# Row sums by accumulating DMAs in one layer of a four-layer graph network, and fewer transposes

## The chip, the cores and the metric

The kernel runs on one core of a Trainium2 chip. The metric is the device time in microseconds (us) of one execution. The core has five instruction streams that run side by side, each in its own order: TensorE (PE, matrix products; loading a stationary operand is shown as PEld), VectorE (DVE), ScalarE (ACT), GpSimd (POOL) and SyncE (SP, which here only issues DMAs).

## The reference

32 samples, each with 512 nodes of 256 features in float32, pass four layers over one 512 x 512 adjacency matrix. Each layer normalises its input, applies relu, and adds its result to the input:

```
for layer in (mha, gat1_gat2, gat_heads4, gat_heads8_prior):
    h = maximum(layernorm(x), 0)
    x = x + layer(h, adj)
```

Layer 0 is masked multi-head attention with 4 heads. Layer 1 is two single-head graph attentions between small dense layers. Layers 2 and 3 are graph attentions with 4 heads of 64 features and 8 heads of 32; layer 3 adds a prior to the logits and ends in a dense layer. For each head of layers 2 and 3:

```
e   = leaky_relu(e_src[i] + e_dst[j])         # e_src, e_dst: one number per node and head
att = softmax(where(adj[i, j], e, -inf), over j)
out[i] = sum_j att[i, j] * v[j]
```

So each head needs for every node i a sum over 512 neighbours j of the weights (the row sum), beside the weighted sum of v.

## The kernel before, in words

The tensors on chip are 128 partitions wide. A sample is four row blocks of 128 nodes. A "block" is a 128 x 512 float32 tile in SBUF; 60 of them (`BLOCKS`) are shared by all work, and 8 PSUM banks of the same shape ("bank") by all matmul results.

Nothing is emitted directly. The functions `layer0` to `layer3` only record instructions (in `Plan.add`, L103 and on) with the tiles they touch, an assumed cost from `cost` (L297) and a due time. `Plan.order` (L148) then goes through all 32 samples' instructions as a list scheduler: at each step it takes, over all engines, the instruction that by the assumed costs can start first, with earlier due times first among equals, and it emits them in that order. Several samples are in work at once. What steers it are constants at the head of the file: `PERIOD` (the spacing of due times), `STARTS`, `PACE` and `LAYERS` (the earliest time of a sample and of its layers), `URGENT` (a shift of the due time of single kinds of tile in single layers) and `BLOCKS`. On the chip each engine keeps the emitted order and waits by semaphores. All recorded instructions carry the line number L261, the one that issues them; so groups are told apart by tile names.

PE works in three forms: full 128 x 128 products, "columns" (up to four products of 32 output rows each side by side, recorded as one unit) and "rows" (two products of 64 contracted rows side by side). A float32 product is two matmul records in the trace, a transpose is one.

The places that the change touches:

- `first_gat` (layer 1) needs two projections of each node, source and destination. Four column products `f1p<-o1,fr1a` leave partial results in 128 rows (the two wanted rows of each of four groups of 32 are repeated through the group). ACT copies them to `part`. Four small products against a 128 x 2 selector `pick` then add up the right rows and turn them so that nodes lie on partitions; DVE copies the eight columns to `sd`.
- `separable` serves layers 2 (`nh` = 4) and 3 (`nh` = 8). A product gives v and, in `e`, both per-node numbers of each head. The source numbers of each row block are transposed (4 transposes into `pt`), copied by ACT to `rT` (nh x 512), written by SP to DRAM (`rd`) and read back as `R`, each head's row repeated on all 128 partitions. Then, for a group of four heads and for each block j of 128 neighbours, ACT forms `p = exp(R + e_dst)` (bias), and DVE `p = max(p, exp(e_dst / ALPHA)) * mask`. Each `p[s]` goes into the column unit that forms `av`. Row sums come in two ways: in group 0 (`added`) DVE adds the four j blocks of a head into `total[s]` and one column unit `sm<-total,ones` sums over partitions at the end; in group 1, which only layer 3 has (its last four heads), a second column unit `sm<-p,ones` follows each of the four `av` units and adds up in PSUM.
- `normalise` sends the sums through DRAM to DVE's reciprocal and back, repeated on partitions (`rc`).
- `norm_t`, at the head of each layer, takes the variance plus epsilon (`ve`, DVE) to the power -1/2 on POOL (`rs`), then `ms` on DVE, `h` on ACT, transposes of `h` on PE and `hT` on ACT. POOL's only other work in the loop is `x<-x,boa` in layer 0.

Of the kernel before, what the change touches and what calls it, by code (L numbers as in the profile page):

```python
# [11 lines left out]
F32 = mybir.dt.float32  # L12
BF16 = mybir.dt.bfloat16
I32 = mybir.dt.int32
AF = mybir.ActivationFunctionType
ALU = mybir.AluOpType
AX = mybir.AxisListType
PSUM = bass.MemoryType.PSUM

P = 128  # L20
N = 512
NT = N // P
D = 256
KD = D // P
HID = 512
KH = HID // P
ALPHA = 0.2
# [5 lines left out]
H3, F3 = 8, 32  # L33
# [5 lines left out]

PERIOD = 51.0
STARTS, PACE = (0.0, 8.0, 36.0, 32.0), 110.0
LAYERS = (0.0, 51.0, 151.0, 201.0)

URGENT = {
    "stats:0": 76, "h:0": 358, "mm:0": 3, "sc:0": 60, "p0:0": -99, "av:0": 39, "stats:1": -269, "pt:1": 119,
    "nd:1": -201, "total:1": 12, "av:1": -22, "e:1": -39, "o2:1": 73, "s:1": -189, "pt:2": 15, "e4:2": -44,
    "total:2": 10, "stats:3": -38, "mv:3": -56, "mm:3": -12, "p3:3": -178, "total:3": -169, "sm:3": 86,
    "s1:3": -16,  # L50
}
BLOCKS, KEEP = 60, 2
KEEP_BANKS = 0
BANKS = ("mm", "av", "sm", "sc", "pt", "fb", "f1p")

# [241 lines left out]
def cost(engine, op, args, kw, out):  # L297

    src = next((kw[k] for k in ("in_", "in0") if k in kw), args[1] if len(args) > 1 else out)
    if not isinstance(src, bass.AP):  # L300
        src = out
    n = 1
    for _, k in (src if op in ("bn_stats", "reduce_max") else out).ap[1:]:
        n *= k
    if engine == "PE":
        return (0.109 if op == "transpose" else max(0.224 if n < 3 else 0.0, n * 0.001676)), 0.165
    pointers = sum(isinstance(kw.get(k), bass.AP) for k in ("bias", "scale"))
    if op == "mul":
        pointers = 1
    if engine == "ACT":  # L310
        busy = 0.05 + 0.000832 * n + 0.093 * pointers + (0.0 if src.tensor.name.startswith(BANKS) else 0.043)
        return busy + (0.093 if "accum_out" in kw else 0.0), 0.12
    if engine == "DVE":
        if op == "reciprocal":
            return 0.06 + 0.0062 * n, 0.085
        if op == "tensor_scalar" and n == N:
            return 0.456, 0.075
        by_pointer = op == "scalar_tensor_tensor" and isinstance(args[2], bass.AP)
        return 0.066 + 0.00105 * n + (0.06 if by_pointer else 0.0), 0.085
    if engine == "POOL":  # L320
        return (1.0 if n < 16 else 0.683), 0.1
    size = 4
    for _, k in (out.ap if out.tensor.name.startswith(("few", "R", "rc", "x")) else src.ap):
        size *= k
    return 0.4, 1.6 + size / 190e3
# [3 lines left out]
def gnn_stack_kernel(ctx: ExitStack, tc: tile.TileContext, a: dict, out: bass.AP):  # L329
# [12 lines left out]
    nc = tc.nc  # L342
# [3 lines left out]
    const = ctx.enter_context(tc.tile_pool(name="const", bufs=1))  # L346

    def T(ap, rearr, **kw):
        return ap.rearrange(rearr, **kw)
# [27 lines left out]
    ident = const.tile([P, P], F32, name="ident")  # L377
# [4 lines left out]
    ones = const.tile([P, P], F32, name="ones")  # L382
# [7 lines left out]

    fr1a = const.tile([P, KH, 32], F32, name="fr1a")
    f1a, r1a = fr1a[:, :, 0:1], fr1a[:, :, 1:2]
    pick = const.tile([P, 2], F32, name="pick")

    w2 = const.tile([P, KD, D + 4 * H2], F32, name="w2")
    w3 = const.tile([P, KD, D + 4 * H3], F32, name="w3")
# [10 lines left out]
    with prep_stack, tc.manual_schedule():  # L407
# [11 lines left out]
        for name in ("bq", "bk"):  # L419
            t = prep.tile([1, D], F32, name=f"{name}r")  # L420
# [32 lines left out]
        H = H2 + H3  # L453
        tests = prep.tile([P, 2 * H + 5], F32, name="tests")
        nc.vector.memset(tests, 0.0)
        for c in range(2):
            nc.vector.tensor_reduce(pick[:, c : c + 1], ident[:, c:P:32], axis=AX.X, op=ALU.add)


        top = prep.tile([P, NT], F32, name="top")  # L460
# [4 lines left out]
        for j in range(NT):  # L465
            pt = pp.tile([P, N], F32, name="adjT", bufs=NT)
# [49 lines left out]
        for w, row in zip((wq, wk), rows):  # L516
            gp = pp.tile([64, N], F32, name="gp", bufs=2)
            for h in range(4):
                c = slice(h * 64, (h + 1) * 64)
# [7 lines left out]
        for n in range(2):  # L527
            for h in range(4):
                c = slice(h * 64, (h + 1) * 64)
# [47 lines left out]
        for k in range(KH):  # L577
            for c in range(2):
                pr = prep.tile([P, HID], F32, name="prf")
                nc.vector.tensor_tensor_reduce(  # L580
                    out=pr, in0=wfc[:, k, :], in1=afc[:, c * HID : (c + 1) * HID], scale=1.0, scalar=0.0,
                    op0=ALU.mult, op1=ALU.add, accum_out=fr1a[:, k, c : c + 1],
# [4 lines left out]
        for k in range(KD):  # L587
            for c in range(2):
                pr = prep.tile([P, HID], F32, name="prf")
                nc.vector.tensor_tensor_reduce(  # L590
                    out=pr[:, :D], in0=wh[:, k, :D], in1=ahd[:, c * D : (c + 1) * D], scale=1.0, scalar=0.0,
                    op0=ALU.mult, op1=ALU.add, accum_out=wh[:, k, D + c : D + c + 1],
# [9 lines left out]
    def pipelined(stack):  # L602

        big = stack.enter_context(tc.tile_pool(name="big", bufs=1))
        psum = stack.enter_context(tc.tile_pool(name="psum", bufs=8, space=PSUM))
        dram = stack.enter_context(tc.tile_pool(name="dram", bufs=6, space=bass.MemoryType.DRAM))
        q = Plan(nc, PERIOD)
        def block(name):

            return q.tile(big, [P, N], name, BLOCKS, keep=KEEP, tag="block")  # L610

        def blocks(name, n):
            return [block(name) for _ in range(n)]

        def bank(name):
            return q.tile(psum, [P, N], name, 8, keep=KEEP_BANKS, tag="bank")

        def small(name, *free):
            return q.tile(big, [P, *free], name, 4)
# [5 lines left out]
        def col(t):  # L625
            return slice(t * P, (t + 1) * P)
# [134 lines left out]
        def first_gat(o1):  # L761
# [4 lines left out]
            part, sd = block("part"), small("sd", NT, 2)  # L766
            f1p = bank("f1p")
# [1 line left out]
                for k in range(KH):  # L769
                    q.tensor.matmul(f1p[k * 32 : k * 32 + 32, :], fr1a[:, k, :], o1[k], start=True, stop=True)  # L770
            q.scalar.copy(part, f1p)
            f1p = bank("f1p")
            for t in range(NT):
                q.tensor.matmul(f1p[:, 2 * t : 2 * t + 2], part[:, col(t)], pick, start=True, stop=True)
            q.vector.tensor_copy(T(sd, "p t c -> p (t c)"), f1p[:, : 2 * NT])
            mx = small("mx", 2)
            q.vector.reduce_max(mx[:, 0:1], sd[:, :, 1], axis=AX.X)
            pt = bank("pt")
            q.tensor.transpose(pt[:1, :P], mx[:, 0:1], ident)
            q.vector.reduce_max(mx[:1, 1:2], pt[:1, :P], axis=AX.X)  # L780
            pt = bank("pt")
            q.tensor.matmul(pt[:, 0:1], ones[:1, :], mx[:1, 1:2], start=True, stop=True)
            nd = small("nd", 3)
# [3 lines left out]
            ew = small("ew", 3, NT)  # L787
# [4 lines left out]
            pt = bank("pt")  # L792
# [4 lines left out]
            p = blocks("p1", NT)  # L797
# [91 lines left out]
        def separable(xt, w, nh, mask, bars):  # L889

            hT = norm_t(xt)
            f = D // nh
            e = small(f"e{nh}", NT, 3 * nh)
            v = blocks("vs", 2)
            for t in range(NT):
                ps = node_major(w, t, hT, nh, D + 2 * nh)
                q.scalar.copy(half(v, t), ps[:, :D])
                q.scalar.copy(e[:, t, : 2 * nh], ps[:, D : D + 2 * nh])
            q.scalar.activation(e[:, :, 2 * nh :], e[:, :, nh : 2 * nh], AF.Exp, scale=1.0 / ALPHA)
            pt = bank("pt")  # L900
            for t in range(NT):
                q.tensor.transpose(pt[:nh, col(t)], e[:, t, :nh], ident)
            rT = block("rT")
            q.scalar.copy(rT[:nh, :], pt[:nh, :])
            rd = q.tile(dram, [H3, N], "rd", 6)
            q.sync.dma_start(rd[:nh, :], rT[:nh, :])
            per = P // f
            for g in range(nh // 4):
                R = blocks("R", 4)
                for s in range(4):  # L910
                    q.sync.dma_start(R[s], rd[4 * g + s : 4 * g + s + 1, :].to_broadcast([P, N]))
                avs = [bank("av") for _ in range(4 // per)]
                added = g == 0
                if added:
                    total = blocks("total", 4)
                else:
                    sm = bank("sm")
                for j in range(NT):
                    p = blocks("p3", 4)
                    for s in range(4):  # L920
                        h = 4 * g + s
                        q.scalar.activation(p[s], R[s], AF.Exp, bias=e[:, j, nh + h : nh + h + 1])
                        q.vector.scalar_tensor_tensor(
                            p[s], p[s], e[:, j, 2 * nh + h : 2 * nh + h + 1], mask[:, j, :], op0=ALU.max, op1=ALU.mult
                        )
                        if added and j:
                            q.vector.tensor_tensor(total[s], first[s] if j == 1 else total[s], p[s], op=ALU.add)
                    if added and not j:
                        first = p
                    st = dict(start=(j == 0), stop=(j == NT - 1))  # L930
                    with q.unit("columns", (0.86 if per == 4 else 1.72) + (0 if added else 0.86)):
                        for s in range(4):
                            h, r0 = 4 * g + s, s % per * f
                            q.tensor.matmul(avs[s // per][r0 : r0 + f, :], half(v, j)[:, h * f : (h + 1) * f], p[s], **st)
                        if not added:
                            for s in range(4):
                                q.tensor.matmul(sm[s * F3 : (s + 1) * F3, :], ones[:, :F3], p[s], **st)
                if added:
                    sm = bank("sm")
                    with q.unit("columns", 0.86):  # L940
                        for s in range(4):
                            q.tensor.matmul(sm[s * F3 : (s + 1) * F3, :], ones[:, :F3], total[s], start=True, stop=True)
                bars(g, avs, sm)

        def layer2(xt):
# [456 lines left out]
```

## Time and profile before

| | us |
|---|---|
| median of 3 runs (4181.32 to 4182.27) | 4181.78 |
| the profiled execution, its own time | 4184.13 |
| its span, from the first to the last instruction | 4182.3 |
| PE busy in the span | 4059.5 |
| DVE busy | 3312.1 |
| ACT busy | 3004.7 |
| POOL busy | 254.8 |

The profile is of one execution. "Busy" is the time in which an engine had at least one instruction under way; for PE the ends of pipelined matmuls are modelled, so the distance between the starts of consecutive groups is the better price of a group. The page cuts the span into 40 equal slices of about 105 us and gives the busy share of each in tenths. The chain of waits is followed back from the last instruction to what released each step. In a timeline line stand the start, the length, the engine, the line of code, the operation, out<-in by tile names, the shapes, and the number of records merged into it.

The DMA groups that matter here, from the list of DMA issues: 384 transfers `R<-rd` of 256 KB from SP, 96 each of the 8 KB transfers of the sums, 64 of `rd<-rT`. POOL issues a single DMA, `adj` (L410, 1024 KB), at the start.

### The profile page before, as it was taken

What the parts mean: (1) busy time and instruction counts of PE and PEld (TensorE: products, weight loads), DVE (VectorE), ACT (ScalarE), POOL (GpSimd) and SP (SyncE); (2) the same over time, 40 slices, a digit from 0 to 9 for tenths busy, and PEclk for the clock granted to TensorE, in tenths of its full rate; (3) what the DMA queues carried; (4) which work ended last, traced back from release to release, by engine and by line L of the source; (5) the groups of instructions that cost most, each with busy time, mean ns of one, the idle gap of its engine ahead of it and who ended that gap; (6) DMA issues with size and microseconds to landing.
All of it is one profiled execution on the core that took longest, in us unless ns stands there. A gap on an engine that the chain in (4) does not pass through costs nothing.

```text
span 4182.3 us, 52787 instructions
## 1 busy us (share of the span) xinstructions
PE 4059.5 (97%) x17862; PEld 2068.7 (49%) x17862; DVE 3312.1 (79%) x7018; ACT 3004.7 (72%) x5970; POOL 254.8 (6%) x263
## 2 busy tenths in 40 slices
PE   5999999999999999999999999999999999999986
PEld 3545454554454554455554455554455554455442
DVE  5388877878877878877879877879877878877876
ACT  3467777766777766777766777776777776787774
POOL 1000000000000000000000000000000000000000
PEclk7999999999999999999999999999999999999998
DMA  2001111111110111110111111111111111111111
GB/s 84 11 21 47 47 47 33 49 52 32 47 51 30 49 52 32 47 52 30 49 52 32 47 52 31 47 52 32 47 52 32 46 52 32 47 52 32 41 42 52
DMA packets 149435, 181.07 MB, mean 43 GB/s; under 512 B 45858, under 2 KB 81572, under 8 KB 149156
## 3 DMA queue, kind: packets, MB, share of 16 engines
q1 hardware_dynamic: 143572, 172.37, 13.5%
q10 hardware_dynamic: 5312, 4.20, 0.3%
q8 instruction: 143, 2.34, 0.2%
q14 instruction: 136, 1.11, 0.1%
q0 software_dynamic: 272, 1.05, 0.1%
HBM read 158.41 MB, written 19.14 MB: 42 GB/s over the span
## 4 chain that ended last, share of the span: by engine, by line
PE 78%; DVE 13%; DMA 4%; ACT 2%; issue 1%; SPq 0%; POOL 0%; DVEq 0%; POOLq 0%
PE mm L261 36%; PE av L261 26%; PE pt L261 6%; PE sc L261 5%; PE sm L261 4%; DVE p L261 3%; DVE total L261 3%; DVE ue L261 2%; DMA rc<-s 2%; DVE o L261 2%; PE f1p L261 1%; DVE oT L261 1%; ACT p L261 1%; DVE x L261 1%; DMA s<-few 1%; DMA R<-rd 1%
## 5 line engine op out<-in xcount | busy, mean ns | idle before, releaser
L261 ACT ACTIVATE p<-R,e 128x512 f32<-128x512 f32 x1536 | 1010.2, 721 | 167.7 <-DMA R<-rd 167.5
L261 DVE SCALAR_TENSOR_TENSOR p<-p,e,mask3T 128x512 f32<-128x512 f32 x1024 | 718.2, 745 | 368.1 <-ACT p L261 367.9
L261 PE MATMUL av<-p,v 128*64 128x512 f32 (+1 forms) x2048 | 689.8, 597 | 1.4 <-DVE p L261 1.4
L261 DVE TENSOR_TENSOR total<-total,p 128x512 f32<-128x512 f32 x832 | 547.2, 680 | 0.0
L261 PE MATMUL av<-p,vs 128*32 128x512 f32 (+1 forms) x3072 | 524.8, 598 | 19.2 <-DVE p L261 19.1
L261 PE MATMUL mm<-W_fc,o 128*128 128x512 f32 x1024 | 467.0, 593 | 0.0
L261 PEld LDWEIGHTS av<-p,v 128*64 128x64 f32 (+1 forms) x2048 | 257.5, 163 | 363.4 <-issue 297.1
L261 POOL TENSOR_TENSOR rs<-ve,mhalf 128x4 f32<-128x4 f32 x128 | 151.0, 1180 | 3764.2 <-DVE ve L261 3593.1
L261 DVE SCALAR_TENSOR_TENSOR p<-p,e,mask1T 128x512 f32<-128x512 f32 x512 | 367.6, 742 | 5.8 <-ACT p L261 5.4
L261 ACT ACTIVATE h<-x,ms,rs 128x256 f32<-128x256 f32 x512 | 269.7, 593 | 128.7 <-DVE ms L261 128.7
L261 DVE TENSOR_TENSOR p<-p,mask0T 128x512 f32<-128x512 f32 x512 | 324.1, 681 | 38.3 <-ACT p L261 38.3
L261 PEld LDWEIGHTS av<-p,vs 128*32 128x32 f32 (+1 forms) x3072 | 135.8, 119 | 346.0 <-issue 239.0
L261 PEld LDWEIGHTS mm<-W_fc,o 128*128 128x128 f32 x1024 | 188.9, 190 | 210.0 <-issue 183.4
L261 DVE TENSOR_TENSOR total<-p,p 128x512 f32<-128x512 f32 x416 | 278.9, 678 | 1.0
L261 ACT ACTIVATE p<-sc 128x512 f32<-128x512 f32 x512 | 262.9, 687 | 7.7 <-PE sc L261 7.7
L261 PE MATMUL mm<-w,hT 128*128 128x272 f32 (+1 forms) x1024 | 262.3, 398 | 1.8 <-ACT hT L261 1.8
L261 PE MATMUL av<-pT,v 128*128 128x512 f32 x512 | 239.9, 593 | 0.5 <-ACT pT L261 0.4
L261 PE MATMUL mm<-o,mlp_w 128*128 128x512 f32 x512 | 228.8, 598 | 0.0
L261 PE MATMUL sc<-qT,kT 64*128 64x512 f32 x1024 | 228.3, 595 | 0.0
L261 PE MATMUL mm<-hT,mlp_w 128*128 128x512 f32 x512 | 225.7, 592 | 0.0
L261 PEld LDWEIGHTS mm<-w,hT 128*128 128x128 f32 x1024 | 188.1, 193 | 54.8 <-ACT hT L261 10.3
L261 ACT COPY sums<-sm 128x512 f32<-128x512 f32 x96 | 55.8, 581 | 195.8 <-PE sm L261 195.7
(187 smaller groups left out, 6076.5 us busy)
## 6 DMA issues: line engine op xcount, KB each, us to landing
R<-rd SPq DMA_DIRECT2D x384, 256.0 KB
x<-in_x_dram SPq DMA_DIRECT2D x32, 512.0 KB
rc<-s SPq DMA_DIRECT2D x128, 128.0 KB
rc<-s SPq DMA_DIRECT2D x256, 64.0 KB
out_dram<-x SPq DMA_DIRECT2D x32, 512.0 KB
s<-sums SPq DMA_DIRECT2D x96, 8.0 KB
few<-s SPq DMA_DIRECT2D x96, 8.0 KB
s<-few SPq DMA_DIRECT2D x96, 8.0 KB
```

Of the source, the lines that this page charges most:

```text
L261: getattr(getattr(self.nc, attribute), op)(*args, **kw)
```

## The change

1. In `separable`, group 1 no longer has its four `sm<-p,ones` units. For j = 1, 2, 3 POOL issues a DMA for each head that adds `p[s]` onto `first[s]`, the block of j = 0 (256 KB, from SBUF to SBUF, `accum_op` add). At the end one unit `sm<-first,ones` sums over partitions.
2. In `separable`, the source numbers go to a tile `es` of their own, NT x nh columns wide, so one transpose replaces four; `rT` is then 16 x 128 or 32 x 128, and the DMA to `rd` puts the rows in order. `e` shrinks by these columns, and ACT makes two small copies per row block where it made one.
3. In `first_gat`, four full transposes of `part` replace the four products with `pick`, and a DVE reduction over the four groups replaces the copy to `sd`. `pick` is gone.
4. In the planner, a DMA on POOL has an assumed cost, and the constants have other values.

```diff
-PERIOD = 51.0
-STARTS, PACE = (0.0, 8.0, 36.0, 32.0), 110.0
-LAYERS = (0.0, 51.0, 151.0, 201.0)
+PERIOD = 54.0
+STARTS, PACE = (0.0, 6.0, 22.0, 46.0), 81.0
+LAYERS = (0.0, 31.0, 185.0, 164.0)
...
-BLOCKS, KEEP = 60, 2
+BLOCKS, KEEP = 59, 2
...
     if engine == "POOL":
+        if op == "dma_start":
+            return 1.2, 3.0
         return (1.0 if n < 16 else 0.683), 0.1
...
-            f1p = bank("f1p")
-            for t in range(NT):
-                q.tensor.matmul(f1p[:, 2 * t : 2 * t + 2], part[:, col(t)], pick, start=True, stop=True)
-            q.vector.tensor_copy(T(sd, "p t c -> p (t c)"), f1p[:, : 2 * NT])
+            pt = bank("pt")
+            for t in range(NT):
+                q.tensor.transpose(pt[:, col(t)], part[:, col(t)], ident)
+            q.vector.tensor_reduce(sd, T(pt, "p (t k c) -> p t c k", k=KH, c=32)[:, :, :2, :], axis=AX.X, op=ALU.add)
...
-            for t in range(NT):
-                q.tensor.transpose(pt[:nh, col(t)], e[:, t, :nh], ident)
-            rT = block("rT")
-            q.scalar.copy(rT[:nh, :], pt[:nh, :])
+            q.tensor.transpose(pt[: NT * nh, :P], es, ident)
+            rT = q.tile(big, [P, P], "rT", 4, tag="turned")
+            q.scalar.copy(rT[: NT * nh, :], pt[: NT * nh, :P])
...
-                        if added and j:
+                        if j and total:
                             q.vector.tensor_tensor(total[s], first[s] if j == 1 else total[s], p[s], op=ALU.add)
-                    if added and not j:
+                        elif j:
+                            q.gpsimd.dma_start(out=first[s], in_=p[s], accum_op=ALU.add)
+                    if not j:
                         first = p
...
-                        if not added:
-                            for s in range(4):
-                                q.tensor.matmul(sm[s * F3 : (s + 1) * F3, :], ones[:, :F3], p[s], **st)
-                if added:
-                    sm = bank("sm")
-                    with q.unit("columns", 0.86):
-                        for s in range(4):
-                            q.tensor.matmul(sm[s * F3 : (s + 1) * F3, :], ones[:, :F3], total[s], start=True, stop=True)
+                sm = bank("sm")
+                with q.unit("columns", 0.86):
+                    for s, b in enumerate(total or first):
+                        q.tensor.matmul(sm[s * F3 : (s + 1) * F3, :], ones[:, :F3], b, start=True, stop=True)
```

`URGENT` has other entries throughout. The rest of the diff is the splitting of `e` into `e` and `es` with the indices that follow from it.

## The prediction

> **What bounds the kernel now.** I read the busy table first, then the slices, then one period of the timeline on TensorE, and last the groups and the chain.
>
> ```profile
> span 4182.3 us, 52787 instructions
> PE 4059.5 (97%) x17862; PEld 2068.7 (49%) x17862; DVE 3312.1 (79%) x7018; ACT 3004.7 (72%) x5970; POOL 254.8 (6%) x263
> ...
> PE   5999999999999999999999999999999999999986
> ...
> PE 78%; DVE 13%; DMA 4%; ACT 2%; issue 1%; SPq 0%; POOL 0%; DVEq 0%; POOLq 0%
> ```
>
> The slices show TensorE full from the second on; only the fill and the drain have gaps. A busy TensorE alone proves little, so I asked for stretches. The period shows in the chain of waits, where the same piece of mm work comes back every 125.14 us (2065.88, 2191.01, 2316.14, ...): one sample per period, 32 samples. In the window from 2000 to 2125.14 PE is busy 124.51 us, DVE 102.47, ACT 93.62, POOL 7.88, at a granted clock of 1.00. TensorE is therefore 99.5% full, and the next engine has 22 us to spare. Outside the steady part, PE idles 49 us before 100 us and 49 us after 4000.
>
> Busy time of a PE group counts the tail of a matmul under the next one, so I price PE work by the distance between starts in the timeline (columns: start, length, then the group and its count):
>
> ```profile
> 2091.59 1.07 PE L261 MATMUL av<-p,vs 128*32 128x512 f32 x8
> 2092.47 1.04 PE L261 MATMUL sm<-p,ones 128*32 128x512 f32 x8
> 2093.33 1.04 PE L261 MATMUL av<-p,vs 128*32 128x512 f32 x8
> 2094.19 1.04 PE L261 MATMUL sm<-p,ones 128*32 128x512 f32 x8
> ...
> 2099.34 1.04 PE L261 MATMUL sm<-total,ones 128*32 128x512 f32 x8
> 2100.20 1.04 PE L261 MATMUL f1p<-o,fr1a 128*32 128x512 f32 x8
> ...
> 2111.74 0.95 PE L261 MATMUL f1p<-pick,part 128*128 128x2 f32 x8
> 2112.55 0.68 PE L261 MATMUL mm<-L_WoT,oT 128*128 128x256 f32 x2
> ...
> 2117.79 0.60 PE L261 MATMUL pt<-ident,ew 128*128 128x128 f32 x4
> 2118.23 0.60 PE L261 MATMUL mm<-L_WoT,oT 128*128 128x256 f32 x2
> 2118.66 0.49 PE L261 MATMUL pt<-ident,e 128*4 128x128 f32 x3
> ```
>
> The next product after that last line starts at 2118.99. An fp32 matmul is two records, so x8 is a unit of four.
>
> **The change part by part, per sample.**
>
> Row sums of layer 3's last four heads: four sm<-p units leave (2092.47 to 2093.33 is 0.86 us), one sm unit comes (2099.34 to 2100.20, 0.86): -2.58 us.
>
> Rows: in layers 2 and 3, four transposes of e each become one. Three take 2118.66 to 2118.99, 0.11 each: six fewer, -0.66 us.
>
> Projections: the eight records with pick take 2111.74 to 2112.55, 0.81 us; four full transposes, priced like those of ew (2117.79 to 2118.23), take 0.44: -0.37 us.
>
> Sum on PE: -3.61 us of 124.51. Changes between full, column and row forms on PE number 304 in the old planned order and 309 in the new; each shows as about 0.11 us (2102.77 + 0.86 = 2103.63, next form at 2103.74): 5 x 0.11, nothing.
>
> Other engines. ACT: the row copies shrink from 4x512 and 8x512 (574 and 559 ns) to 16x128 and 32x128 (estimated 250, between the 128x16 copy at 179 ns and the 128x256 at 382): -0.6 us; eight e copies become sixteen at about 175 ns: +1.4. ACT goes from 93.6 to about 94.4, hidden under PE as long as PE is above that. DVE: the reduce in place of an 8-column copy (157 ns) costs perhaps 0.1 more; 102.6. SP: the same number of transfers; the e rows leave in 16 or 32 short rows in place of 4 or 8 long ones, over the same 8 or 16 KB. Transfers of 8 KB between SBUF and DRAM in the chain take 1.4 to 1.7 us; this wait sits behind R, whose consumers come later. I cost it at nothing, a microsecond of latency at worst.
>
> **The added wait.** Twelve accumulating transfers of 256 KB per sample go onto POOL's queue, three in a row into each of four blocks. The first four wait for PE's av of key block 0 (it reads what they overwrite), the next eight for the transfer before in the same block, and PE's sm unit waits for the last four. No row of before shows such a transfer. The bounds: issue 0.92 us, from the one transfer that POOL issued (L410 adj, 918 ns); above, 0.92 x 2494/1001 = 2.29, if it is stretched like the slowest rs against the fastest. Landing from 1.4 us (s<-few, 8 KB) to 10.2 us (adj, 1 MB, four times the size). I take 0.92, and about 3 us by size between these two; both ends stay for the range.
>
> [...] rs on POOL, the same 128x4 each time, took 1001 / 1178 / 2494 ns (min, median, max): something stretches POOL. [...]
>
> What covers it: in the new planned order I added up PE work between av of key block 0 of the last four heads and their sm unit. It is 37 to 39 us in every group from the second to the 29th. The chain of twelve needs, with two rs between, 12 x 0.92 + 2.4 + 3 = 16.4 us; at a landing of 10.2, 3 x 10.2 + 4 x 0.92 + 1.2 = 35.5; at an issue of 2.29, 27.5 + 5 + 3 = 35.5. Each end alone is covered. Only both ends together (27.5 + 5 + 10.2 = 43) pass 37. No PE instruction is then late; what is late first is what stands behind on POOL.
>
> Queued behind the waiting transfers: in every second sample one rs (a norm of another sample) stands behind one transfer, another behind six. Their transposes of h stand 11 to 12 and 16 to 17 us of PE work after av. Needed for the second: 6 x 0.92 + 2 x 1.18 + 0.16 (ms) + 0.59 (first h) = 8.6; at a landing of 10.2, 10.2 + 2 x 0.92 + 1.18 + 0.75 = 14; at an issue of 2.29, 13.7 + 5 + 0.75 = 19.5, 3 us late. x<-x,boa stands before or after the block of transfers.
>
> DMA bandwidth: 384 x 256 KB more (101 MB, read twice) on 16 engines that are busy 14%; cover enough.
>
> **Fill and drain.** The new constants move the order: in steady state a sample's first transposes and last products lie about 450 us of PE work apart, against 384 before, so more samples are open at once; this gives cover and needs blocks (59 in place of 60). I see no sign for the fill. In the drain, after about 4060, the chain runs through DVE p and total, and PE is a third idle: there the cut brings nothing. So I count 30 samples, not 32: 30 x 3.61 = 108.3. The last two groups have only 9 and 6 us of PE work ahead of their sm, but the old kernel ran 6.5 us of av and sm after the last p (4154.2 to 4160.7), where the new one has issue, landing and one unit (0.9 + 3 + 0.9): even.
>
> **Sum**: the profiled execution took 4184.13 us (span 4182.3). 4184.1 - 108.3 = 4075.8. The median of the runs shown is 2.35 lower than the profiled execution; so 4073.5, say 4074.
>
> **Rivals.**
>
> A, the forecast: the cover holds and PE stays the bound, at about 121.5 us per sample. Fill and drain of the new order and the steady idle (0.6 us a sample) may each move 10 to 15: 4055 to 4100. Chance 0.72.
>
> B, a part comes back as a stall: rs behind six transfers is 3 us late in every second sample, 15 x 3 = 45: 4074 + 45 = about 4119. For it speaks the spread of rs; against it the medians and that DVE's own chain (ve, rs, ms, h) rarely holds PE today (PE waited 15.8 us for h in the whole span). Chance 0.14.
>
> C, slower: the twelve transfers, one after another on POOL, outlast their cover, and sm takes over as PE's wait. Its place is the sm unit of the last four heads, its price 30 us per microsecond beyond 37; from 37 + 3.6 = 40.6 us for the twelve it eats the whole gain. With both ends, 43 us: 4074 + 6 x 30 = 4254. Against it: both ends would have to hold, each far from the nearest row. Chance 0.09.
>
> D, the work goes and the time doesn't: the new order leaves PE idle for what it saved, say on p of DVE, which is at 102.5 of a period of 121.5 and has to deliver in bursts. About 4180. Against it: 19 us to spare in each period. Chance 0.05.
>
> **How the numbers follow.** The likeliest is A, 4074. The range takes A's own and B's: 4050 to 4130, leaving out C, D and a little of each other, about 2 in 10. The measurement tells 0.2%, about 8 us, from no change: faster A and B, 0.86; same D, 0.05; slower C, 0.09.
>
> **What would show it.** Right: the sm<-p group at a quarter of its count; PE about 3.6 us less busy per period of about 121.5 us and still over 99% full there; no PE wait for a DMA at sm; POOL up by some 11 us per sample in issues. Wrong: PE waiting at sm for a POOL transfer, or at pt<-h; POOL issues of over 2 us; DVE instructions longer than 745 and 680 ns while POOL issues.

## The result and the profile after

| | before | after |
|---|---|---|
| median, us | 4181.55 (4180.15 to 4182.27, 4 runs) | 4221.2 (4217.98 to 4225.6, 4 runs) |
| profiled execution, own time | 4184.13 | 4225.6 |
| its span | 4182.3 | 4223.4 |
| PE busy | 4059.5 | 4001.1 |
| PE idle (span less busy) | 122.8 | 222.3 |
| one sample (mean of 22 periods) | 125.20 | 127.22 |

The ratio is 1.0096 [1.0078, 1.0113]: the changed kernel is slower by about 40 us, where 108 fewer were forecast. A period is taken here from the start of one sample's `part<-f1p` on ACT to the next sample's, from the 6th to the 28th.

The page of the kernel after: span, busy table, PE's slices, two DMA queues, and the chain.

```profile
span 4223.4 us, 52074 instructions
...
PE 4001.1 (95%) x16774; PEld 2052.9 (49%) x16774; DVE 3312.9 (78%) x7016; ACT 2994.6 (71%) x6226; POOL 669.1 (16%) x647
...
PE   5999999999999999999999999999999999999986
...
q0 software_dynamic: 55568, 101.74, 14.3%
q1 hardware_dynamic: 144596, 172.37, 13.1%
...
PE 72%; ACT 7%; DVE 7%; DMA 7%; issue 4%; POOL 1%; SPq 1%; DVEq 0%; ACTq 0%; POOLq 0%
```

PE is less busy, as it should be, but by 58 us and not by 32 x 3.61 = 115.5; and it idles 99.5 us more. These two make the whole difference: -115.5 + 57 + 99.5 = +41, and the spans differ by 41.1. DVE did not grow and ACT fell by 10 us. The adding transfers (all of q0 but one) take a share of the DMA engines as large as all of SP's transfers. By place: the 6th `part` starts 15 us earlier than before, the 22 periods after it cost 44 us more, and from the 28th on 12 more.

The list of waits of the kernel after (waiter, releaser: us in all, times, longest) says what PE waited for:

```profile
PE mm L261 <- DVE oT L261: 67.0, 14, 11.1
PE pt L261 <- DVE rs L261: 48.7, 15, 4.1
...
PE sm L261 <- DMA p<-p: 1.4, 3, 0.7
```

The last line answers the prediction's fear: PE hardly ever waits for the adding transfers. It waits for two things that no part of the change touches, each once in two samples. In before, mm waits for oT 31 times, nearly always 0.6 us (7.4 once, in the drain), and pt waits for no rs of DVE:

```profile
PE mm L261 <- DVE oT L261: 29.2, 31, 7.4
```

**The gap ahead of mm<-woT.** Timeline of the kernel after (start, length, engine, group; in brackets the idle time before it and its releaser), put together from PE, DVE and SP:

```profile
2320.61 0.39 SPq L261 DMA_DIRECT2D s<-few  x1
2321.94 3.64 SPq L261 DMA_DIRECT2D R<-rd  x8
2325.68 3.48 SPq L261 DMA_DIRECT2D rc<-s  x4
2327.41 2.74 PE L261 MATMUL av<-pT,v 128*128 128x512 f32 x6
2333.85 1.29 DVE L261 TENSOR_TENSOR oT<-raw,rc 128x512 f32<-128x512 f32 x2 [6.94 <-DMA rc<-s]
2334.69 6.44 PE L261 MATMUL mm<-woT,oT 128*128 128x256 f32 x16 [4.54 <-DVE oT L261]
```

SP could have read the reciprocals back (rc) once `s<-few` was through, but in the new order eight transfers R of another sample, 2 MB, stand ahead of it. DVE then waits 6.94 us for rc, and PE 4.54 for DVE. In the order of before, no rc stands directly behind R; in the order of after this happens 14 times.

**The gap ahead of pt<-rs**, put together in the same way with ACT and POOL:

```profile
2242.67 0.86 POOL L261 DMA_DIRECT2D p<-p  x1 [0.69 <-DVE p L261]
2243.05 0.63 SPq L261 DMA_DIRECT2D rd<-rT  x1
2247.52 2.56 SPq L261 DMA_DIRECT2D R<-rd  x4
2249.89 0.95 PE L261 MATMUL sm<-ones,total 128*128 128x1 f32 x8
2252.33 1.33 ACT L261 ACTIVATE p<-R,e 128x512 f32<-128x512 f32 x2 [3.28 <-DMA R<-rd]
2253.09 1.41 DVE L261 SCALAR_TENSOR_TENSOR p<-p,e,mask1T 128x512 f32<-128x512 f32 x2 [3.70 <-ACT p L261]
2254.42 0.18 DVE L261 RECIPROCAL rs<-sm 128x4 f32<-128x4 f32 x1
2254.74 0.92 PE L261 MATMUL pt<-ident,rs 128*128 128x128 f32 x4 [2.93 <-DVE rs L261]
```

Here PE needs a reciprocal of 0.18 us (`rs1` in the code of layer 1), whose input sm PE had finished at 2250.84, 3.6 us before it ran. It stands on DVE behind a p of layer 2, this behind ACT's p, this behind R, and R behind `rd<-rT`, the write of the e rows. From its issue to that of R 4.47 us pass. In before, where R follows rd directly (63 times), it is 1.47 in the median and 2.10 at most; in after, 16 of 36 such times take over 2.5. Adding transfers were under way at the time, and the window (columns below) has a DMA share of 1.09; packets are counted where they start, so a share can pass 1:

```profile
2242.00:2244.00 2.00, 2.00 (x10) 1.09 (x9) 2.00 (x4) 1.03 (x8) 0.86 (x1) 1.00 1.09 182
```

**The clock after a gap.** The windows of the kernel after around the first gap (columns: stretch, its length, busy time of PE, PEld, DVE, ACT, POOL, then granted clock, DMA share, GB/s):

```profile
2330.00:2332.00 2.00, 0.15 (x1) 0.00 (x0) 0.00 (x0) 2.00 (x4) 0.00 (x0) 1.00 1.00 232
2332.00:2334.00 2.00, 0.00 (x0) 0.00 (x0) 0.15 (x1) 2.00 (x4) 0.00 (x0) 0.86 0.18 57
2334.00:2336.00 2.00, 1.31 (x3) 1.16 (x4) 2.00 (x4) 2.00 (x5) 0.00 (x0) 0.50 0.04 8
2336.00:2338.00 2.00, 2.00 (x6) 1.55 (x6) 2.00 (x4) 1.23 (x3) 0.00 (x0) 0.50 0.00 0
2338.00:2340.00 2.00, 2.00 (x7) 1.55 (x6) 0.46 (x1) 0.00 (x0) 0.00 (x0) 0.50 0.00 0
2340.00:2342.00 2.00, 2.00 (x8) 1.41 (x7) 1.26 (x3) 0.00 (x0) 0.00 (x0) 0.94 0.00 0
```

Two things are to be seen. The DMA share is 1.00 while rc waits: 2 MB are passing. And once PE works again, the granted clock is 0.50 for 5.6 us more (6.83 in all, 1.26 of it still in the gap). So a gap is paid twice: 4.5 us of idling, and 5.6 us in which PE counts as busy and does half the work (the records of mm<-woT start 427 ns apart in the median at 0.50, elsewhere 216), 2.8 us lost. Over 1000 to 2000 us the mean clock is 0.98, before 1.00. Added up over all of PE's busy time, half of each stretch at 0.50, the slow clock costs 70.8 us in after and 23.4 in before (almost all of the latter in the fill and the drain). That is 47 of the 57 us; the other 10 are work that did not fall quite as far as counted.

### The profile page after: what moved, and what is told of

The parts are those of the page before. It is cut to its first block, busy times and chain, and to the rows that moved or that the text cites. A ratio compares the mean times of both kernels' runs of the same rounds, so it can differ in the third digit from the quotient of the medians.

```text
span 4223.4 us, 52074 instructions
## 1 busy us (share of the span) xinstructions
PE 4001.1 (95%) x16774; PEld 2052.9 (49%) x16774; DVE 3312.9 (78%) x7016; ACT 2994.6 (71%) x6226; POOL 669.1 (16%) x647
## 3 DMA queue, kind: packets, MB, share of 16 engines
q0 software_dynamic: 55568, 101.74, 14.3%
## 4 chain that ended last, share of the span: by engine, by line
PE 72%; ACT 7%; DVE 7%; DMA 7%; issue 4%; POOL 1%; SPq 1%; DVEq 0%; ACTq 0%; POOLq 0%
PE mm L261 34%; PE av L261 25%; PE pt L261 6%; PE sc L261 4%; DVE p L261 3%; DMA R<-rd 3%; ACT p L261 3%; PE sm L261 3%; DMA rc<-s 2%; DVE total L261 2%; ACT h L261 1%; ACT s L261 1%; ACT e L261 1%; POOL rs L261 1%; DMA rd<-rT 1%
## 5 line engine op out<-in xcount | busy, mean ns | idle before, releaser
L261 ACT ACTIVATE p<-R,e 128x512 f32<-128x512 f32 x1536 | 993.3, 727 | 97.4 <-DMA R<-rd 91.4
L261 PE MATMUL av<-p,v 128*128 128x512 f32 (+1 forms) x2048 | 705.1, 602 | 1.3 <-DVE p L261 1.2
L261 POOL TENSOR_TENSOR rs<-ve,mhalf 128x4 f32<-128x4 f32 x128 | 215.3, 1683 | 2785.1 <-DVE ve L261 2522.8
L261 PE MATMUL av<-p,vs 128*32 128x512 f32 (+1 forms) x3072 | 500.3, 598 | 13.7 <-DVE p L261 13.7
L261 POOL DMA_DIRECT2D p<-p x384 | 354.2, 1201 | 667.6 <-PE av L261 514.7
L261 PEld LDWEIGHTS av<-p,v 128*128 128x128 f32 (+1 forms) x2048 | 265.8, 167 | 368.9 <-issue 321.3
L261 DVE SCALAR_TENSOR_TENSOR p<-p,e,mask1T 128x512 f32<-128x512 f32 x512 | 349.5, 744 | 70.0 <-ACT p L261 69.8
L261 DVE TENSOR_TENSOR oT<-raw,rc 128x512 f32<-128x512 f32 x128 | 87.6, 692 | 226.5 <-DMA rc<-s 218.7
L261 ACT COPY v<-mm 128x512 f32<-128x512 f32 (+1 forms) x320 | 156.0, 500 | 147.5 <-PE mm L261 146.6
L261 DVE BATCH_NORM_STATS2 stats<-x 128x6 f32<-128x256 f32 x512 | 187.6, 407 | 55.3 <-DMA x<-in_x_dram 55.3
```

The source lines that it names most:

```text
L261: getattr(getattr(self.nc, attribute), op)(*args, **kw)
```

## The experiments

What the traces suggest, my theory: two causes together. The new planned order puts latency-bound work (rc, the reciprocal) behind transfers of another sample, and the adding transfers, dearer than their bytes, fill the DMA engines and stretch these waits. Rivals: the order alone; the transfers alone; and POOL's work slowing DVE. Unless told otherwise each kernel has the code and the constants of after and the planned order of after; only what its diff shows is different. The edits that move instructions go through a method that takes the planner's finished order and puts single steps elsewhere in their engine's queue, ahead of emission; every dependence stays. In the traces the queues of SP, DVE, ACT and POOL of e1, e3, e4, e8, e9, e12 and e13 hold the same steps as those of after, with 112 places changed on SP, 32 on DVE and 34 on ACT where a move is named, and no other.

| | median us | ratio to before | one sample |
|---|---|---|---|
| after | 4221.2 | 1.0096 [1.0078, 1.0113] | 127.22 |
| e1_small | 4143.7 | 0.9912 [0.9895, 0.9929] | 124.25 |
| e2_copy | 4148.2 | 0.9915 [0.9898, 0.9931] | 124.6 |
| e3_rcfirst | 4199.9 | 1.0043 [1.0026, 1.006] | 126.27 |
| e4_recip | 4212.8 | 1.0069 [1.0052, 1.0086] | 126.65 |
| e5_oldconst | 4634.6 | 1.1079 [1.1061, 1.1098] | |
| e6_transposes | 4220.4 | 1.0087 [1.007, 1.0104] | 124.73 |
| e7_newconst | 4609.8 | 1.1018 [1.0999, 1.1036] | |
| e8_both | 4181.8 | 0.9999 [0.999, 1.0009] | 125.51 |
| e9_small_both | 4124.1 | 0.9855 [0.9838, 0.9871] | 124.13 |
| e10_pooladd | 4531.9 | 1.0839 [1.0821, 1.0857] | 136.18 |
| e11_pooladd_both | 4500.9 | 1.0758 [1.0741, 1.0776] | |
| e12_three | 4147.0 | 0.9911 [0.9895, 0.9928] | 124.50 |
| e13_small_three | 4095.3 | 0.9791 [0.9775, 0.9808] | 122.60 |

Of the forecasts on record below, only that of e1 came out as the theory had it. e2 came out 17 us below its range; e8 lies between its two; e4 and e11 came out as long as their rivals had it; the others came out longer than the theory had it. Where a move mended a gap, it gave less than the gap was priced at, because the next wait then came up.

**e1_small: the same instructions, small transfers.**

```diff
-q.gpsimd.dma_start(out=first[s], in_=p[s], accum_op=ALU.add)
+q.gpsimd.dma_start(out=first[s][:, :16], in_=p[s][:, :16], accum_op=ALU.add)
```

> The changed kernel, with each of POOL's accumulating transfers cut to the first 16 of 512 columns (so the row sums of layer 3's last four heads are wrong from column 16 on); every engine's order stays as it is. Theory 'crowding and order': the transfers fill the DMA engines and so delay rd and R, behind which VectorE's reciprocal rs waits; that gap (about 14 gaps of 3.1 us idle plus 1.7 us of lowered clock, 67 us in all) goes, the gap before mm<-woT stays: about 4150. Rival 'order alone' (the new constants, not the transfers): no change, 4215 to 4225. Rival 'POOL's queue' (issues hold rs of the norms): no change either, since as many issues remain, POOL busy about as before.

4143.7, 77 us under after. The gap ahead of pt<-rs is gone, that ahead of mm<-woT stays (14 times, about 4 us). The size of the transfers is a cause of its own, since not one instruction was moved or left out. POOL's queue is not how it works: POOL's issues took 1.67 us in the mean in e1 against 1.20 in after, its rs 1655 ns against 1683. And the write of the e rows is short again: issue to issue 1.92 us in the median, one of 36 over 2.5.

**e2_copy: a copy in place of the addition.** The row sums are left out. The constant `mask3T` is made as m3 times m3 in place of m3 times `mask1T`, so that it has no zeros; the work is the same.

```diff
-q.gpsimd.dma_start(out=first[s], in_=p[s], accum_op=ALU.add)
+q.gpsimd.dma_start(out=first[s], in_=p[s])
```

> The changed kernel with plain copies in place of adding ones, full size, same order (row sums and the zeros of layer 3's mask are left out, mask3T is kept above zero). The adding transfers' packets took 14.3% of 16 engines' span for 101.7 MB, against 13.1% for 172.4 MB on SP's queue. If adding costs a second read, the share falls to 7 to 8%, landing from 5.4 to about 3 us, and the rs gap shrinks: 4165 to 4200. If only the number of bytes written counts: share and time as in the changed kernel, 4215 to 4225.

4148.2, level with e1, whose runs spread over 14 us. Its page has the queue and the issues (KB each, median us to landing):

```profile
q0 software_dynamic: 30992, 101.74, 6.6%
...
p<-p POOLq DMA_DIRECT2D x384, 256.0 KB, 2.8
```

and the page of after has for the same bytes 55568 packets, 14.3%, and

```profile
p<-p POOLq DMA_DIRECT2D x384, 256.0 KB, 5.4
```

So it is the addition, not the bytes: 2.2 times the DMA engines' time and twice the time to landing. In after, 0.143 x 4223 / 32 = 19 us of every sample's 127 would have all 16 engines full with it, if it came in one piece.

**e3_rcfirst: on SP, rc moved ahead of the eight R.**

```diff
-            for step in self.order():
+            for step in self.moved(self.order()):   # SP: rc before the R that stand directly ahead of it
```

> The changed kernel with one move on SP: where rc<-s transfers stand behind the eight R<-rd of another sample's layer 3, they are issued ahead of them (every second sample); all else in order. Theory 'crowding and order': the wait of mm<-woT for oT for rc is made by these 2 MB in front; about 14 gaps of 4.3 us idle plus 3 us of lowered clock go, R comes 3.5 us later: 4120 to 4150, and that gap is under 1 us. Rival 'the accumulating transfers make rc late': no change, 4215 to 4225.

4199.9, 21 under after. The mm<-woT gap is gone; but 14 new gaps of 36.3 us in all stand ahead of av<-pT, and 40.6 ahead of pt<-rs are as they were. R now starts later, and what needs R is late.

**e4_recip: on DVE, the reciprocal moved ahead of one to three p of layer 2** (the same method, another pair of kinds).

> The changed kernel with one move on VectorE: the reciprocal rs1 of layer 1 ahead of the one to three layer-2 p instructions directly before it, which wait for R. Theory 'crowding and order': the gap at pt<-rs (14 gaps of 3.1 us idle plus 1.7 us of lowered clock) goes, the other stays: about 4150. Rival 'the late R itself holds TensorE': the gap only moves to av of layer 1 or 2, 4200 to 4225.

4212.8, 8 under after. The pt<-rs gap is gone, 30.0 us ahead of pt<-h are new (24 times), and the mm<-woT gap stays. Taking one late thing away brings up the next.

**e5_oldconst, e6_transposes and e7_newconst** were to part the change into its pieces, each planned anew: the code of after with the constants of before; the transposes alone (row sums on PE as in before) with the constants of before; the code of before with the constants of after. All have 59 blocks.

```diff
-PERIOD = 54.0        # e5, e6: and STARTS, PACE, LAYERS, URGENT, all of before
+PERIOD = 51.0
...
-PERIOD = 51.0        # e7: and the others, all of after
+PERIOD = 54.0
```

> The changed kernel's code under the old constants (PERIOD, STARTS, PACE, LAYERS, URGENT of before; 59 blocks), planned anew. In this order the rc transfers no longer stand behind eight R. Theory 'the constants cost about 70 us by that gap, the adding transfers about 77 by crowding': only the second is left, 4115 to 4155. Rival 'crowding hits whatever order': as slow as the changed kernel, 4200 to 4240.

> The fewer transposes for rows and projections alone: old constants (59 blocks), row sums of layer 3's last four heads on TensorE as before, no transfer on POOL. The prediction's price is 0.66 + 0.37 us per sample on TensorE, times 30 to 32 samples: 4183 - 31 to 33, 4145 to 4155 against 4183. Rival 'the row transfer with short rows is late on VectorE's path': 4170 or more.

> The kernel before under the new constants (59 blocks), planned anew; no other edit. If the new constants by themselves make an order with gaps of 4 us on TensorE, 4230 to 4270; if the gaps come only from what the changed code puts into that order (no rc stands behind R here), 4170 to 4195.

4634.6, 4220.4 and 4609.8. Their times part nothing: an order planned with the constants of the other code came out 1% to 11% longer, in e5 and e7 with many gaps (PE is busy 910 and 951 us of 1000). What the new constants cost by themselves, and what the new code does to the order, is so not shown. Only e6 says something: its PE is busy 123.35 us a period against 124.52, so the fewer transposes take 1.17 us off PE where I had counted 1.03. The period falls by only 0.47 (124.73 against 125.20) because PE idles 0.69 us more in it, and the fill is 45 us longer (6th `part` at 768.6, before 723.4); both are the order again.

**e8_both: the moves of e3 and e4.**

> The changed kernel with both moves (rc ahead of eight R on SP, the reciprocal ahead of layer 2's p on VectorE). If the gains of the two moves add (21 and 8 us): 4185 to 4195, with 2 us gaps at av<-pT and pt<-h left, since R and the norms are late by the adding transfers. If either gap was only a cover of the other: more than 40 us, 4150 to 4180.

4181.8 over 10 runs, 39 under after and level with before. The two moves give 10 us more together than one by one (21 + 8), at a spread of 17 us among e8's runs. What is left shows in ACT's timeline of this kernel:

```profile
2060.67 0.72 ACT L286 ACTIVATE p<-R,e 128x512 f32<-128x512 f32 x1 [2.87 <-DMA R<-rd]
2061.30 2.03 ACT L286 COPY pT<-pt 128x512 f32<-128x512 f32 x4
```

A copy pT that PE waits for stands on ACT behind a p of layer 3, and this waits for R: the same pattern on a third queue (39.9 us, 14 times ahead of av<-pT).

**e9_small_both: e8 with the transfers of e1.**

> The changed kernel with the transfers cut to 16 of 512 columns (row sums wrong from column 16 on) and with both moves (rc ahead of eight R, the reciprocal ahead of layer 2's p). In e1 one gap was left, 14 times about 4 us idle and 3 us of lowered clock before mm<-woT. If that is all that stands between e1 and the prediction's sum: 4060 to 4090, a pitch of 121 to 122 us per sample. Rival 'the sum on TensorE itself was wrong' (the leaving units and transposes were worth less than 3.61 us): no gap of over 1 us is left, yet 4110 or more.

4124.1, 58 under e8; 39.5 us ahead of av<-pT are left. The order costs even where the transfers are small, and the transfers cost even where two places of the order are mended. Neither rival that names one cause alone stands.

**e10_pooladd and e11_pooladd_both: the same additions as GpSimd instructions**, in the same place of POOL's queue, without and with the moves of e8.

```diff
-q.gpsimd.dma_start(out=first[s], in_=p[s], accum_op=ALU.add)
+q.gpsimd.tensor_tensor(first[s], first[s], p[s], op=ALU.add)
```

> The changed kernel with the twelve adding transfers per sample replaced by twelve additions on GpSimd itself (first = first + p, 128x512), in the same place on POOL, all orders kept. Theory 'the bytes of the adding transfers crowd the DMA engines': no such bytes, so as e1, 4140 to 4155, if an addition takes about 1.5 us (128x256 takes 0.73). Rival 'POOL's additions and VectorE hold each other': VectorE instructions of 0.68 us get longer or rs gets late, 4170 to 4250.

> As e10, with both moves. If e9's account holds and POOL's additions cost nothing else: 4060 to 4100, ahead of both kernels. If the additions hold VectorE: within 20 us of e8 (4182) or above.

4531.9 and 4500.9. The groups of e10, DVE's largest and POOL's new one (busy, mean ns):

```profile
L261 DVE SCALAR_TENSOR_TENSOR p<-p,e,mask3T 128x512 f32<-128x512 f32 x1024 | 885.4, 907 | 127.0 <-ACT p L261 125.9
L261 POOL TENSOR_TENSOR p<-p,p 128x512 f32<-128x512 f32 x384 | 625.8, 1661 | 544.4 <-PE av L261 522.8 <-DVE p L261 20.4 <-DVE ve L261 1.2
```

The same DVE group in after:

```profile
L261 DVE SCALAR_TENSOR_TENSOR p<-p,e,mask3T 128x512 f32<-128x512 f32 x1024 | 722.9, 747 | 124.5 <-ACT p L261 123.4
```

745 ns in before, 747 with the adding transfers, 907 with POOL's additions; DVE's busy time grows from 3312.9 to 3674.4 us. So the third rival is wrong for the change and right for this way around it: with POOL issuing, this group took what it took before, with POOL computing 22% more in the mean.

**e12_three: a third move, on ACT, pT ahead of the p of layer 3.** Nothing is left out. Here the three queues are mended first, and the emitted order is then made anew from the five queues.

```diff
+queues["SP"] = pull(queues["SP"], lambda t: kind(t, "rc"), lambda t: kind(t, "R"))
+queues["DVE"] = pull(queues["DVE"], lambda t: kind(t, "rs1"), lambda t: kind(t, "p3") and t.layer == 2)
+queues["ACT"] = pull(queues["ACT"], lambda t: kind(t, "pT"), lambda t: kind(t, "p3"))
```

> The changed kernel, nothing left out, with three moves: rc ahead of eight R (SP), the reciprocal ahead of layer 2's p (VectorE), and the four pT copies ahead of the one or two layer-3 p directly before them (ScalarE), which in e8 waited 2.9 us for R while TensorE waited 2.85 us for pT, 14 times. If queue order behind late R is what is left: 14 x (2.85 idle + 1.5 to 2.5 of lowered clock) = 60 to 75 less than e8 (4182), 4105 to 4125, ahead of both kernels. If another consumer then waits in its place, as after each of the moves before: 4150 to 4185.

4147.0, 0.9911 [0.9895, 0.9928]: faster than both kernels, by 0.9% against before, with the change's own code and three kinds of steps moved. PE's wait for oT is back (19.4 us, 14 times ahead of mm<-woT), and 32.2 us ahead of pt<-h are left.

**e13_small_three: e12 with the transfers of e1.**

> e12 with the transfers cut to 16 of 512 columns (row sums wrong from column 16 on). If the prediction's sum on TensorE was right and only gaps stood against it: no gap of over 1 us in steady state, a pitch of 120.5 to 122 us, 4060 to 4085. If the pitch stays at 124 with no gap, the sum itself was wrong.

4095.3, 52 under e12. Its page and one window of its steady part (columns as above):

```profile
span 4093.7 us, 52148 instructions
...
PE 3951.5 (97%) x16774; PEld 2021.7 (49%) x16774; DVE 3303.6 (81%) x7016; ACT 2989.2 (73%) x6226; POOL 667.2 (16%) x647
```

```profile
1000.00:2000.00 1000.00, 990.22 (x4253) 509.58 (x4253) 836.20 (x1776) 751.64 (x1570) 170.26 (x161) 1.00 0.17 45
```

The same window of the kernel after, with the same instructions on PE:

```profile
1000.00:2000.00 1000.00, 969.75 (x4133) 499.25 (x4131) 804.58 (x1705) 731.72 (x1531) 165.41 (x160) 0.98 0.29 69
```

e13 gives PE the same 16774 records as after in 49.6 us less of busy time, 43 of them by the clock (27.5 us lost against 70.8), and in 80 less of idle time. Both parts of the loss belong to the gaps. The forecast for e13 was 4060 to 4085 with no gap of over 1 us; gaps of up to 3.2 us ahead of mm<-woT are left.

All kernels that bear on it, side by side (PE's own waits between 400 and 3950 us, summed from the lists of waits; idle is span less busy):

| | before | after | e8 | e12 | e13 |
|---|---|---|---|---|---|
| PE's waits, 400 to 3950 | 22 | 111 | 85 | 68 | 38 |
| PE idle, whole span | 122.8 | 222.3 | 193.9 | 176.8 | 142.2 |
| PE busy | 4059.5 | 4001.1 | 3979.0 | 3972.6 | 3951.5 |

The same by sample, the mean of the 22 periods, which leaves out fill and drain ("lost" is half of PE's busy time at a granted clock of 0.50, from the trace's clock records):

| us | before | after | e6 | e8 | e12 | e13 |
|---|---|---|---|---|---|---|
| one sample | 125.20 | 127.22 | 124.73 | 125.51 | 124.50 | 122.60 |
| PE idle | 0.69 | 4.11 | 1.38 | 3.08 | 2.43 | 1.23 |
| PE busy | 124.52 | 123.12 | 123.35 | 122.42 | 122.07 | 121.37 |
| of this, lost to the slow clock | 0.00 | 1.93 | 0.08 | 1.04 | 0.75 | 0.16 |
| busy less lost | 124.52 | 121.18 | 123.27 | 121.38 | 121.32 | 121.22 |

The last row is PE's work. It is 3.1 to 3.3 us less in after, e8, e12 and e13, whatever their time does. In after, 3.3 us of work go, 3.4 of idling and 1.9 of slow clock come: the 2.0 that a sample takes longer.

## Why the prediction was wrong, step by step

- **The sum on PE, -3.61 us a sample: held, within a tenth.** PE's work a sample falls by 3.3 us in after and in e13. With small transfers and three moves the kernel comes to 4095.3, inside the 4055 to 4100 of A, though at 122.6 us a sample and not 121.5. In after the gain is paid back elsewhere.
- **The added wait: held.** PE waited 1.4 us at sm in the whole span; the issue is 0.86 to 0.92 us typically (mean 1.20), the landing 5.4, within the bounds though not the 3 that I took. Rival C fell with that, by its own condition. Two signs of being wrong did show on POOL, 25 of 384 issues over 2 us and an rs of 1683 ns in the mean against 1180 (4.3 us at most, beyond the 2494 ns that gave my bound). They are not the cause: e1 has both, 86 issues and 1655 ns, and takes 77 us less.
- **"SP: the same number of transfers ... I cost it at nothing" failed, and so did the sentence it leans on, "16 engines that are busy 14%; cover enough".** I took a mean share for room. The adding transfers come in bursts and fill all the engines: in the window 2242 to 2244 of after, where the e rows are on their way, the share is 1.09. The write of the rows and its wait then take 4.47 us in place of 1.47. e2, whose rows are as short but whose transfers only copy, has 1.92 in the median; so the short rows cost about half a microsecond, within the one that I had allowed, and the other 2.5 are the transfers. Price of the transfers' size in all: 77 us in the order of after, 58 with two moves, 52 with three. I also priced the addition as a copy of its bytes ("about 3 us by size"), though my own line on bandwidth has it read twice; no run shows the reads themselves, only the time to landing: 2.8 us for the copy, 5.4 for the addition.
- **"More samples are open at once; this gives cover" failed, and is the larger miss in reasoning.** I had looked in the new order at PE's distances and at what stands behind POOL's waiting transfers, not at what stands behind SP's R, DVE's p and ACT's p, though the new plan re-sorts every queue. Open samples give cover to PE, but they also put one sample's short, urgent step behind another's long wait. Price by the three moves: 74 us with full transfers (4221.2 to 4147.0), 48 with small ones (4143.7 to 4095.3).
- **A term that the sum lacked: the clock after a gap.** 47 us of PE's busy time (1.93 of every sample's 127.22). In my rivals I priced a stall at its length; here all 22 stalls of 3.1 to 5.0 us in the steady part of after (400 to 3900 us), and three of five of 2.3 to 2.9, cost 1.4 to 3.0 more, half of what PE worked in 3.41 or 6.83 us at a clock of 0.50.
- **Rival B** (rs late on POOL) did not bind in after; ahead of pt<-h there are 14.7 us, most of it one wait in the fill. Its place shows once the others are mended, 30.0 us in e4, 32.2 in e8 and in e12, 1.3 each, but not its mechanism: ahead of each of these 72 waits the rs took 2.5 us, and it had waited for DVE's ve, not behind transfers. **Rival D** named the right kind of outcome, PE idle for what it saved, at 4180, and the wrong waiter: DVE had its 19 us a period to spare and kept them, but behind single waits an average says nothing.

The two costs overlap: transfers and order make each other's waits longer, so 77 and 74 are not to be added. Together they are 4221.2 - 4095.3 = 126 us, which is more than the 108 of the gain.

Left open: why pt<-h comes late in e8 and e12 and not in e13 (the rs there took 2.5 us, such as that at 2267.40 in e12 with 2.54, but the spread of rs is the same in both kernels: 1446 and 1448 ns in the median, 4.3 us at most); how the 21 us between e13 and 4074 divide (mm<-woT still waits 15 times for 20.0 us, and PE's work fell 0.3 us a sample short of the sum); how much of the order is due to the constants and how much to the code; and why the orders of e5 and e7 are so much worse.

## What to carry to other kernels

When a change comes with a new planned order, read every engine's queue for short steps that stand behind a wait of other work, and do it on the DMA queues first; the order was worth 74 us here, where the work removed was worth 108. Price an accumulating DMA by what it takes of the DMA engines while it runs (here 2.2 times what a copy took), not by its bytes or by the mean share, and look for what small transfer with a waiter behind it runs at the same time. Price a gap of TensorE at its length plus the slow clock behind it, where the trace shows one: in the runs here it stood behind 81 of 85 gaps of 3 us and more and behind 47 of 72 of 2 to 3.

## What the runs showed of the hardware

- Adding 256 KB from SBUF to SBUF by DMA took 5.4 us to landing, copying them 2.8; 14.3% of the 16 engines against 6.6, and 55568 packets against 30992.
- An adding transfer of 16 columns (8 KB) still took 3.0 us to landing, and as many packets as one of 256 KB (55568 in both kernels).
- TensorE's granted clock fell to 0.50 after gaps of 2.93 and 4.54 us in after (1.26 us ahead of the end of the second), for 3.41 and 6.83 us, and after one of 2.61 in e12, for 3.41; after before's gaps, 29 of 0.63 to 0.79 us between 400 and 3900, it did not. The steady parts (400 to 3900 us) of before, after, e1 to e4, e8, e9, e12 and e13 together have 84 gaps of 0.5 to 1.5 us with no other gap close by (10 us before, 8 behind), and no half clock behind any; 8 of 21 gaps of 1.5 to 2 us have it, 47 of 72 of 2 to 3, 18 of 21 of 3 to 3.5, and 63 of 64 longer ones. Each time it lasted 3.41 or 6.83 us.
